# First layer's beginning: a constant tile on TensorE, the first context in four loads, two query groups behind the first scores

## The chip, the core and the metric

The kernel runs on one core of one Trainium2 chip. A core has several engines that run side by side, each with its own queue of instructions: TensorE (PE in the profile; its weight loads are listed apart as PEld), VectorE (DVE), ScalarE (ACT), GpSimd (POOL), and SyncE (SP), which in this kernel issues the transfers (DMAs). They hand over to one another by semaphores. Matrix products go from SBUF, the on-chip memory, to PSUM, a set of banks from which ACT and DVE copy the results out. The metric is the device time of one execution in microseconds (us); the shorter the better.

## The reference

Four layers follow one another on `x` of 8 batches, 100 rows and 512 columns, with a context of 8 batches, 361 rows and 512 columns. Only the first layer's head matters here. The first layer is an attention with 32 query heads of 16 columns and 8 key heads, each of which serves four query heads:

```python
q = hidden_state @ Wq + bq
k = encoder_hidden_state @ Wk + bk
v = encoder_hidden_state @ Wv + bv
q = q.reshape(b, l, KVH, GROUPS, HD).transpose(0, 2, 3, 1, 4)
...
scores = jnp.einsum('bkgld,bksd->bkgls', q, k) * scale
scores = scores + encoder_attention_mask[:, :, None, :, :]
attn = jax.nn.softmax(scores, axis=-1)
out = jnp.einsum('bkgls,bksd->bkgld', attn, v)
...
out = out @ Wo + bo
x = out + hidden_state
```

A normalization of the rows ends the layer. Layer 2 is a recurrent one, layer 3 a second attention, layer 4 two more attentions and two dense products. All values are 32-bit floats.

## The kernel before

**The loop.** The first layer walks over the eight batches `b`. In each it walks over seven row tiles `t` (`row_tiles`, six of 115 rows and one of 110). The 800 rows of a batch are, for one half of the key heads after the other, 4 query groups of 100 rows: row `r` belongs to group `r % 400 // 100`. So row tile 0 (rows 0 to 114) holds rows of groups 0 and 1, row tile 1 (115 to 229) of groups 1 and 2, and row tile 2 (230 to 344) of groups 2 and 3.

**The pieces, by function.**

- `context(b)` (L235) issues the load of a batch's context, turned so that its columns lie on the partitions: tile `cx`, four chunks of 128 columns in one DMA (L238, 722 KB). For `b == 0` it issues the query weights `wq` as well (the helper `load`, L91, 1024 KB) and the first 200 columns of the turned input, `xT` (L247, 400 KB).
- `keys(b)` (L251) multiplies the four chunks of `cx` with the key weights `wk`, one chunk after the other, into the PSUM tile `pk`; ACT writes the result with its bias to `kT` (L255).
- `queries(b, g)` (L289) makes one query group for two batches from `wq` and `xT` in the PSUM tile `pq`. ACT writes the half for the even key heads (L300), DVE that for the odd ones (L301), both into the tile `qz`. The even half is rows 0 to 399, the odd half rows 400 to 799.
- `masks(b)` (L303) issues the mask's rows for all seven row tiles. A row tile runs over the end of a head's 100 rows, so each takes two DMAs (L312). There are six buffers for the seven tiles.
- `key_values(b)` (L257) makes the values: three row blocks of `cx` times the weights `wv`, into the PSUM tile `pw`, with the bias `bv` added by DVE (L281). For `b == 0` it also issues a string of loads: `wv` (256 KB), `bv`, the second context, the rest of `xT` (L265, 1200 KB), the rows `x` (L269), `wo` and three row vectors.
- `scores(b, t, qz)` (L318) makes four score tiles `sc` of one row tile, one for each pair of key heads (L325). They have four PSUM banks.
- `softmaxed` (L333) adds the mask and finds the row minimum of the negated scores on DVE (L337), and takes exponentials on ACT (L341).
- `turned` (L344) transposes the exponentials of the row tile before on TensorE (`pt`, L349); the copies to `at` are ACT's for three of the four pairs (L229) and DVE's for the fourth (L231). The transposes have two PSUM banks.
- `values` (L377) multiplies the exponentials with the values and finishes the rows.

**What sets the order.** Within `tc.manual_schedule` (L451) the engines PE, DVE and ACT keep the order in which the program calls them. SP and POOL are not listed: a planner places their instructions when the program is built. All DMAs of the head go through SP's one queue. They use eight semaphores in turn, and an issue waits until the DMA that had its semaphore before has landed, that is the eighth before it.

**The head's order on TensorE.** `keys(0)`; `queries(0, 0)` to `queries(0, 3)`; then, in the loop for `b == 0`: the scores of row tile 0, the values' product (`key_values(0)`), the scores of row tile 1, the transposes of row tile 0, the scores of row tile 2, and so on. At `t == 2` and `t == 6` come query groups of the next two batches. The PSUM tiles `pk`, `pq`, `pw` and some later ones share a tag, "av", with two banks.

A matrix product of 32-bit floats appears in the trace as two instructions: the four products of `pk` are listed as x8, the sixteen of the four query groups as x32.

Of the kernel before, what the change touches and what calls it, by code (L numbers as in the profile page):

```python
# [10 lines left out]
F32 = mybir.dt.float32  # L11
# [5 lines left out]
P = 128  # L17
B, L, C, S = 8, 100, 512, 361
T = B * L
NC = C // P  # L20
# [36 lines left out]
def kernel(ctx: ExitStack, tc: tile.TileContext, d: dict, out: bass.AP):  # L57
    nc = tc.nc
# [20 lines left out]
    def row_bcast(dst, name, parts, lo=0, n=None):  # L79
        at, size = RV_AT[name]  # L80
        n = size if n is None else n
        nc.sync.dma_start(out=dst, in_=d["rvec"][0:1, at + lo : at + lo + n].to_broadcast([parts, n]))
# [5 lines left out]
    def load(pool, name, k, n, tag, lo=None):  # L88
        t = pool.tile([P, k, n], F32, tag=tag, name=tag)
        src = d[name] if lo is None else d[name][:, lo : lo + n]  # L90
        nc.sync.dma_start(out=t, in_=src.rearrange("(c p) n -> p c n", p=P))  # L91
        return t
# [108 lines left out]
    with ExitStack() as es:  # L201
        p1 = es.enter_context(tc.tile_pool(name="l0_1", bufs=1))
        p2 = es.enter_context(tc.tile_pool(name="l0_2", bufs=2))
        p4 = es.enter_context(tc.tile_pool(name="l0_4", bufs=4))
        ps = es.enter_context(tc.tile_pool(name="l0_ps", bufs=2, space=PSUM))
# [3 lines left out]

        keys3 = (0, KB, S - KB)  # L210

        wk = load(p1, "L0_xattn_Wk", NC, P, "wk")
        qmask = p1.tile([P, 2], F32, tag="qmask", name="qmask")
        nc.sync.dma_start(out=qmask, in_=d["qmask"])
# [8 lines left out]
        wv = bv = wq = wo = xT = bo = gamma = beta = None  # L223
# [11 lines left out]
        def context(b):  # L235

            cx = p2.tile([P, NC, S], F32, tag="cx", name="cx")
            nc.sync.dma_start(  # L238
                out=cx, in_=d["ctxT"][:, b * S : (b + 1) * S].rearrange("(c p) s -> p c s", p=P)
            )  # L240
            contexts[b] = cx
            nonlocal wq, xT
            if b == 0:
                wq = load(wpool, "L0_xattn_Wq", NC, C, "w")
                xT = p1.tile([P, NC, T], F32, tag="xT", name="xT")
                rows = d["xT"].rearrange("(c p) t -> p c t", p=P)
                nc.sync.dma_start(out=xT[:, :, : 2 * L], in_=rows[:, :, : 2 * L])  # L247
            if b == 2:
                factors.extend(load(wpool, f"L2_xattn_w_{j}", NC, C, "w") for j in "qk")

        def keys(b):  # L251
            cx = contexts[b]
            pk = ps.tile([P, 512], F32, tag="av", name="pk")
            mm_sum(pk[:, :S], [(wk[:, c, :], cx[:, c, :]) for c in range(NC)])
            nc.scalar.activation(kT[:, b, :], pk[:, :S], AF.Identity, bias=col("L0_xattn_bk", 0), scale=1.0)  # L255

        def key_values(b):  # L257
            cx = contexts.pop(b)
            nonlocal wv, bv, wo, bo, gamma, beta
            if b == 0:  # L260
                wv = load(p1, "L0_xattn_Wv", NC, P, "wv")
                bv = p1.tile([P, P], F32, tag="bv", name="bv")
                row_bcast(bv, "L0_xattn_bv", P)
                context(1)
                nc.sync.dma_start(  # L265
                    out=xT[:, :, 2 * L :], in_=d["xT"].rearrange("(c p) t -> p c t", p=P)[:, :, 2 * L :]
                )
                for i in range(B):
                    nc.sync.dma_start(out=x[i], in_=d["x"][i])  # L269
                wo = load(wpool, "L0_xattn_Wo", NC, C, "w")  # L270
                bo = p1.tile([L, C], F32, tag="bo", name="bo")
                row_bcast(bo, "L0_xattn_bo", L)
                gamma = p1.tile([L, C], F32, tag="gamma", name="gamma")
                row_bcast(gamma, "L0_xattn_gamma", L)
                beta = p1.tile([L, C], F32, tag="beta", name="beta")
                row_bcast(beta, "L0_xattn_beta", L)
            pw = ps.tile([P, 512], F32, tag="av", name="pw")
            for k, lo in enumerate(keys3):
                mm_sum(pw[:KB, k * P : (k + 1) * P], [(cx[:, c, lo : lo + KB], wv[:, c, :]) for c in range(NC)])
            for k in range(3):  # L280
                nc.vector.tensor_tensor(  # L281
                    v[:, b, k, : 8 * HV].rearrange("p (h e) -> p h e", e=HV)[:, :, :16],
                    pw[:KB, k * P : (k + 1) * P].rearrange("p (h e) -> p h e", e=16),
                    bv[:KB].rearrange("p (h e) -> p h e", e=16),
                    ALU.add,
                )
            nc.gpsimd.memset(v[: 3 * KB - S, b, 2, :], 0.0)
# [15 lines left out]
        def masks(b):  # L303

            tiles = []
            for r0, n in row_tiles:
                mk = p2.tile([QR, S], F32, tag="mask", name="mask", bufs=6)
                tiles.append(mk)
                done, lo = 0, r0 % L
                while done < n:  # L310
                    m = min(n - done, L - lo)
                    nc.sync.dma_start(  # L312
                        out=mk[done : done + m], in_=d["mask_Bx1xSxS2_ff0"][b, 0, lo : lo + m]
                    )
                    done, lo = done + m, 0
            return tiles

        def scores(b, t, qz):  # L318
# [106 lines left out]
        def advance():  # L425
            for g in list(steps):
                try:
                    next(g)
                except StopIteration:
                    steps.remove(g)  # L430
# [19 lines left out]
        ordered = {mybir.EngineType.PE, mybir.EngineType.DVE, mybir.EngineType.Activation}  # L450
        with tc.manual_schedule(engines=ordered):  # L451
            context(0)
            keys(0)
            for g in range(4):
                queries(0, g)
            before = None

            for b in range(B):
                mk = masks(b)
                ats = [p2.tile([KB, 3, PROWS], F32, tag="at", name="at", bufs=4) for _ in range(NPAIR)]  # L460
                y = p2.tile([L, C], F32, tag="y", name="y", bufs=1)
                for t in range(len(row_tiles)):
                    banks = scores(b, t, qzs[b - b % 2])
                    prs = []
                    if t == 1 and b > 0:
                        prs = [softmaxed(t, banks[p], mk) for p in range(NPAIR)]
                        last = values(b - 1, 1, *late)
                        next(last)
                        start(last)
                    copies = []  # L470
                    if before is not None:
                        copies = [turned(before[0], p, before[1][p], before[2][p]) for p in range(2)]
                        for copied in copies:
                            copied()
                    prs = prs or [softmaxed(t, banks[p], mk) for p in range(NPAIR)]
                    if b > 0:
                        next(adding, None)
                    advance()
                    if t == 0:
                        key_values(b)  # L480
                        if 0 < b < B - 1:
                            context(b + 1)
                    if t == 4 and b + 1 < B:
                        keys(b + 1)
                    if t in (2, 6) and b - b % 2 + 2 < B:
                        queries(b - b % 2 + 2, b % 2 * 2 + t // 6)
                    if before is not None:
                        for p in range(2, NPAIR):
                            turned(before[0], p, before[1][p], before[2][p])()
                    before = (t, prs, ats)  # L490
                    if b == B - 2 and t == 6:
                        first_rows()
                    if t == 4:
                        start(values(b, 0, ats, y))
                late = (ats, y)
            for p in range(NPAIR):
                if p == 0:
                    fold_chunk(0, *factors, wqk_d, ps.tile([P, 512], F32, tag="av", name="pf"), p2)
                turned(before[0], p, before[1][p], before[2][p])()
            start(values(B - 1, 1, *late))  # L500
            while steps:
                advance()
            assert len(added) == 2
# [6 lines left out]
    with ExitStack() as es:  # L510
        p1 = es.enter_context(tc.tile_pool(name="l1_1", bufs=1))
        pb = es.enter_context(tc.tile_pool(name="l1_2", bufs=2))
        ps = es.enter_context(tc.tile_pool(name="l1_ps", bufs=2, space=PSUM))
# [470 lines left out]
        with tc.manual_schedule(engines=L1_ORDERED):  # L984
# [11 lines left out]
            for n in range(NU * STEPS + 1):  # L996
                u, c, i = n // STEPS, n % STEPS // 4, n % 4
# [33 lines left out]
                if n == 3 * STEPS - 3:  # L1031
# [4 lines left out]
                    for src in (wqk_d, wvo_d):  # L1036
                        t = wpool.tile([P, NC, C], F32, tag="w", name="w")
# [19 lines left out]
    ps = ctx.enter_context(tc.tile_pool(name="l3_ps", bufs=2, space=PSUM))  # L1057
# [589 lines left out]
```

## Time and profile before

| what | value |
|---|---|
| runs of the kernel | 2767.51, 2770.15 and 2777.99 us, median 2770.15 |
| the profiled execution | 2770.51 us |
| its span, first to last instruction | 2768.7 us, 40339 instructions |
| TensorE's busy share of the span | 96% |
| first matmul | starts at 8.53 us |
| first query product | starts at 13.32 us |
| first scores | start at 18.87 us |

Times within the profile count from the first instruction. The span is a little shorter than the execution's own time. A row of the timeline gives the start of a group of equal instructions, how long it lasted, the engine, the line, the operation, the tiles written and read, and the number of instructions; in brackets stands how long the engine was idle before it, and what ended that. A wait for several semaphores is put down to the one that came last, and since DMAs share semaphores, the DMA that is named there can be another one of the same semaphore.

SP's issues of the head, from the timeline (start us, us):

```profile
0.74 0.41 SPq L66 DMA_DIRECT2D pv<-in_pvec  x1
1.20 0.42 SPq L82 DMA_DIRECT2D alpha<-in_rvec  x1
1.66 0.43 SPq L91 DMA_DIRECT2D wk<-in_L_xattn_Wk  x1
2.13 0.51 SPq L214 DMA_DIRECT2D qmask<-in_qmask  x1
2.68 0.43 SPq L238 DMA_DIRECT2D cx<-in_ctxT  x1
3.16 0.51 SPq L91 DMA_DIRECT2D w<-in_L_xattn_Wq  x1
3.71 0.51 SPq L247 DMA_DIRECT2D xT<-in_xT  x1
4.26 11.07 SPq L312 DMA_DIRECT2D mask<-in_mask_Bx1xSxS_ff  x12
15.37 0.40 SPq L91 DMA_DIRECT2D wv<-in_L_xattn_Wv  x1
15.81 0.51 SPq L82 DMA_DIRECT2D bv<-in_rvec  x1
16.37 0.43 SPq L238 DMA_DIRECT2D cx<-in_ctxT  x1
16.84 0.51 SPq L265 DMA_DIRECT2D xT<-in_xT  x1
21.86 0.68 SPq L312 DMA_DIRECT2D mask<-in_mask_Bx1xSxS_ff  x2
```

The first seven DMAs have the queue to themselves. Twelve mask DMAs follow, spread over 11 us, then those of `key_values(0)`; the seventh row tile's masks stand last, as their buffer comes free with the first row tile.

### The profile page before, as it was taken

How to read it: one execution, taken by the hardware profiler on the slowest of the kernel's cores; microseconds unless marked ns; L12 is line 12 of the kernel's file. 1: busy time of each engine (PE TensorE's matmuls, PEld its weight loads, DVE VectorE, ACT ScalarE, POOL GpSimd, SP SyncE). 2: the span in 40 equal slices, each digit the busy share in tenths (PEclk: the TensorE clock that was granted, in tenths of full speed). 3: DMA queues.
4: the chain of work that ended last, by engine and by line, in shares of the span. 5: the costliest groups of instructions: out<-in, count | busy, mean ns of one | idle time of the engine just before them, and what ended most of it. 6: DMA issues, size and time to landing. Idle time of an engine off the chain costs nothing.

```text
span 2768.7 us, 40339 instructions
## 1 busy us (share of the span) xinstructions
PE 2668.2 (96%) x14572; PEld 2147.3 (78%) x14572; DVE 1459.1 (53%) x3779; ACT 964.1 (35%) x2224; POOL 843.8 (30%) x1090
## 2 busy tenths in 40 slices
PE   8999889898989999999999999999999999999999
PEld 5666566675667899877799987789987789997688
DVE  4788367877425544436544436544444754443733
ACT  5777344553312333321333330233340133332211
POOL 2000144532103223255322236222326332324312
PEclk9999989999999999999999999999999999999999
DMA  7432433254205100045200025300005410004300
GB/s 226 122 101 69 146 101 116 89 149 132 64 5 155 42 23 22 7 112 149 69 22 23 1 63 156 110 19 22 12 11 144 133 48 22 22 4 132 126 13 13
DMA packets 142745, 207.52 MB, mean 75 GB/s; under 512 B 44910, under 2 KB 78158, under 8 KB 142290
## 3 DMA queue, kind: packets, MB, share of 16 engines
q1 hardware_dynamic: 142546, 204.94, 25.7%
q8 instruction: 116, 1.90, 0.3%
q14 instruction: 83, 0.68, 0.1%
HBM read 199.29 MB, written 5.61 MB: 74 GB/s over the span
## 4 chain that ended last, share of the span: by engine, by line
PE 73%; DVE 3%; ACT 1%; issue 1%; POOL 0%; DVEq 0%; POOLq 0%; ACTq 0%
PE pz L96 20%; PE sl L96 9%; PE su L96 6%; PE pk L1152 6%; PE pa L96 6%; PE pq L96 5%; PE po L1336 5%; PE pp L96 4%; PE pu L96 3%; PE pt L1267 2%; PE pl L96 2%; PE sc L96 2%; PE po L96 0%; PE pe L96 0%; DVE st L744 0%
## 5 line engine op out<-in xcount | busy, mean ns | idle before, releaser
L96 PE MATMUL pz<-at,cr 121*128 121x248 f32 (+3 forms) x2688 | 579.7, 358 | 0.0
L96 PEld LDWEIGHTS pz<-at,cr 121*128 121x128 f32 (+1 forms) x2688 | 471.0, 189 | 42.3 <-ACT at L1270 3.4
L1216 POOL TENSOR_TENSOR ss<-qz 128x248 f32<-128x248 f32 x96 | 68.1, 709 | 631.4 <-PE su L96 487.1
L1152 PE MATMUL pk<-q,wb 128*128 128x400 f32 x512 | 189.9, 501 | 1.1 <-PE pq L96 1.1
L750 POOL TENSOR_TENSOR st<-st,r 128x800 f32<-128x800 f32 x64 | 112.0, 1750 | 236.0 <-DVE st L744 199.0
L96 PE MATMUL pa<-qz,wa 128*128 128x400 f32 x512 | 178.8, 500 | 0.0
L1301 ACT ACTIVATE pr<-su,nm 124x362 f32<-124x362 f32 x96 | 54.1, 564 | 328.4 <-DVE nm L1298 328.4
L96 PE MATMUL sl<-ts,ss 128*124 128x181 f32 x768 | 155.6, 324 | 0.3
L1079 DVE COPY qz<-pz 128x496 f32<-128x496 f32 (+1 forms) x112 | 70.9, 633 | 139.7 <-PE pz L96 139.0
L96 PEld LDWEIGHTS pa<-qz,wa 128*128 128x128 f32 x512 | 95.5, 190 | 63.0
L1077 ACT COPY qz<-pk 128x400 f32<-128x400 f32 x128 | 63.0, 492 | 231.1 <-PE pk L1152 231.1
L96 PEld LDWEIGHTS sl<-ts,ss 128*124 128x124 f32 x768 | 116.8, 186 | 19.4 <-issue 11.4
L1152 PEld LDWEIGHTS pk<-q,wb 128*128 128x128 f32 x512 | 93.5, 190 | 48.5 <-ACT qz L1077 3.7
L1270 ACT COPY at<-pt 121x372 f32<-121x372 f32 (+1 forms) x208 | 89.0, 473 | 113.3 <-PE pt L1267 113.1
L349 PEld LDWEIGHTS pt<-ident,pr 115*121 115x121 f32 (+1 forms) x672 | 83.2, 185 | 56.5 <-ACT at L229 29.2
L744 DVE TENSOR_TENSOR_SCAN st<-wd,a 128x808 f32<-128x808 f32 x64 | 117.1, 1830 | 15.2 <-PE py L755 13.4
L1077 ACT COPY qz<-pz 128x496 f32<-128x496 f32 (+1 forms) x112 | 60.5, 540 | 183.2 <-PE pz L96 182.7
L1306 ACT ACTIVATE pr<-pr,ss 124x362 f32<-124x362 f32 (+1 forms) x208 | 118.3, 594 | 8.7 <-DVE ss L1304 7.8
L341 ACT ACTIVATE pr<-pr,nm 115x361 f32<-115x361 f32 (+1 forms) x224 | 115.2, 592 | 10.4 <-DVE nm L337 10.4
L1121 DVE TENSOR_TENSOR tu<-sl,tu 124x181 f32<-124x181 f32 x96 | 33.4, 348 | 157.4 <-PE sl L96 157.3
L1372 DVE TENSOR_TENSOR aT<-pa,u 128x400 f32<-128x400 f32 x64 | 36.8, 575 | 142.5 <-PE pa L96 123.7
L337 DVE CUSTOM_DVE_ANT_0 pr<-sc,mask 115x361 f32<-115x361 f32 (+1 forms) x224 | 106.1, 531 | 11.0 <-PE sc L325 10.8
(360 smaller groups left out, 5640.6 us busy)
## 6 DMA issues: line engine op xcount, KB each, us to landing
va<-vd SPq DMA_DIRECT2D x64, 404.0 KB
wa<-in_L_xattn_wq SPq DMA_DIRECT2D x64, 256.0 KB
wb<-in_L_xattn_wk SPq DMA_DIRECT2D x64, 256.0 KB
wa<-in_L_xattn_wv SPq DMA_DIRECT2D x64, 256.0 KB
wb<-in_L_xattn_wo SPq DMA_DIRECT2D x64, 256.0 KB
u<-pd SPq DMA_DIRECT2D x64, 200.0 KB
cr<-in_ctxR SPq DMA_DIRECT2D x16, 726.0 KB
cx<-in_ctxT SPq DMA_DIRECT2D x16, 722.0 KB
```

The lines of the kernel that those rows point to most:

```text
L96: nc.tensor.matmul(dst, lhsT=lt, rhs=r, start=(i == 0), stop=(i == len(pairs) - 1))
L337: nc.vector.tensor_tensor_reduce(out=pr[:n], in0=sc[:n, :S], in1=mk[t][:n], scale=-1.0, scalar=FLT_MAX, op0=ALU.add, op1=ALU.min, accum_ou ...
L341: nc.scalar.activation(pr[:n], pr[:n], AF.Exp, bias=nm[:n], scale=-1.0)
L349: nc.tensor.transpose(pt[:KB, k * n : (k + 1) * n], pr[:n, lo : lo + KB], ident[:n, :n])
L744: nc.vector.tensor_tensor_scan(st.rearrange("p q b l -> p (q b l)"), wd.rearrange("p q t -> p (q t)"), a, 0.0, ALU.mult, ALU.add,)
L750: nc.gpsimd.tensor_tensor(st, st, rc.unsqueeze(1).to_broadcast([P, 4, UB, L]), ALU.mult)
L1077: nc.scalar.copy(o, i)
L1079: nc.vector.tensor_copy(o, i)
L1152: nc.tensor.matmul(pk[:, :HT], lhsT=wk[:, c * P : (c + 1) * P], rhs=q, start=True, stop=True)
L1270: nc.scalar.copy(at[:, :, o : o + r], pt[:KB, : 3 * r].rearrange("p (k r) -> p k r", r=r))
L1306: nc.scalar.activation(pr[:r, : S + 1], pr[:r, : S + 1], AF.Copy, scale=ss[:r])
L1336: nc.tensor.matmul(po[:, c], lhsT=left[k][:, c * P : (c + 1) * P], rhs=right[k], start=True, stop=True)
```

## The change

Four edits, all in the first layer.

1. A tile `ones` of 128 by 128 is filled by DVE, and TensorE multiplies it with itself 16 times (`WARM`) into a PSUM tile of the tag "av", between `context(0)` and `keys(0)`. Nothing reads the result.
2. `context(0)` loads the first context in four DMAs, one for each chunk of 128 columns, where there was one. Later contexts keep one DMA.
3. `wv` and `bv` are issued in `masks(0)`, behind the DMAs of the first row tile and ahead of those of the second, where they stood in `key_values(0)` behind all masks.
4. Only query groups 0 and 1 are made ahead of the loop. Group 2 is made in row tile 0 and group 3 in row tile 1, each behind the row tile's own softmax in the program's order: on TensorE group 2 stands between the scores of row tile 0 and the values' product, and group 3 between the first and the second half of the transposes of row tile 0; on ACT and DVE their evictions stand behind the softmax of row tile 0 and of row tile 1.

```diff
+        WARM = 16
+        ones = p1.tile([P, P], F32, tag="ones", name="ones")
+        nc.vector.memset(ones, 1.0)
         wk = load(p1, "L0_xattn_Wk", NC, P, "wk")
...
-            nc.sync.dma_start(
-                out=cx, in_=d["ctxT"][:, b * S : (b + 1) * S].rearrange("(c p) s -> p c s", p=P)
-            )
+            src = d["ctxT"][:, b * S : (b + 1) * S].rearrange("(c p) s -> p c s", p=P)
+            for c in range(0, NC, 1 if b == 0 else NC):
+                cs = slice(c, c + 1 if b == 0 else NC)
+                nc.sync.dma_start(out=cx[:, cs], in_=src[:, cs])
...
             if b == 0:
-                wv = load(p1, "L0_xattn_Wv", NC, P, "wv")
-                bv = p1.tile([P, P], F32, tag="bv", name="bv")
-                row_bcast(bv, "L0_xattn_bv", P)
                 context(1)
...
                     done, lo = done + m, 0
+                if wv is None:
+                    wv = load(p1, "L0_xattn_Wv", NC, P, "wv")
+                    bv = p1.tile([P, P], F32, tag="bv", name="bv")
+                    row_bcast(bv, "L0_xattn_bv", P)
...
             context(0)
+            pk = ps.tile([P, 512], F32, tag="av", name="warm")
+            for _ in range(WARM):
+                nc.tensor.matmul(pk[:, :P], lhsT=ones, rhs=ones, start=True, stop=True)
             keys(0)
-            for g in range(4):
+            for g in range(2):
                 queries(0, g)
...
                     if b > 0:
                         next(adding, None)
+                    elif t < 2:
+                        queries(0, t + 2)
                     advance()
```

More of the change, by code (lines that the diff above doesn't have):

```diff
@@ L258, in key_values @@
             cx = contexts.pop(b)
-            nonlocal wv, bv, wo, bo, gamma, beta
+            nonlocal wo, bo, gamma, beta
             if b == 0:
-                wv = load(p1, "L0_xattn_Wv", NC, P, "wv")
-                bv = p1.tile([P, P], F32, tag="bv", name="bv")
-                row_bcast(bv, "L0_xattn_bv", P)
                 context(1)
@@ L305, in masks @@
             tiles = []
+            nonlocal wv, bv
             for r0, n in row_tiles:
```

## The prediction

> **What bounds the kernel, and the head of it.** I read the page first (busy shares), then a table of stages, then the head's timeline, engine by engine. Page, then stages (us; busy time of PE, PEld, DVE, ACT, POOL with instruction counts; granted clock; DMA share; GB/s):
>
> ```profile
> PE 2668.2 (96%) x14572; PEld 2147.3 (78%) x14572; DVE 1459.1 (53%) x3779; ACT 964.1 (35%) x2224; POOL 843.8 (30%) x1090
> ...
> 0.00:24.00 24.00, 15.47 (x86) 11.83 (x86) 5.50 (x22) 6.07 (x11) 4.00 (x8) 1.00 0.77 236
> 24.00:40.00 16.00, 14.20 (x96) 9.80 (x96) 9.59 (x36) 13.29 (x30) 0.00 (x0) 1.00 0.77 237
> 40.00:310.00 270.00, 253.77 (x1895) 164.86 (x1893) 202.41 (x866) 187.10 (x408) 11.44 (x15) 1.00 0.36 103
> ```
>
> TensorE bounds the whole. The change touches only the first 31 us or so. In the first 24, PE idles 8.53; from 24 to 40 ACT is the busiest after PE (13.29 of 16) and PE idles 1.8. So more than about 10 us cannot be won, and whatever is won early must pass 24 to 31 us, where PE waits for ACT. PE's timeline there (start, us, what; in brackets idle before it):
>
> ```profile
> 8.53 4.95 PE L96 MATMUL pk<-cx,wk 128*128 128x361 f32 x8 [8.53 <-DMA cx<-in_ctxT]
> 13.32 5.63 PE L96 MATMUL pq<-xT,w 128*128 128x200 f32 x32
> 18.87 0.88 PE L325 MATMUL sc<-kT,qz 32*115 32x361 f32 x8
> 19.68 2.88 PE L96 MATMUL pw<-wv,cx 128*121 128x128 f32 x24
> 22.49 0.88 PE L325 MATMUL sc<-kT,qz 32*115 32x361 f32 x8
> ...
> 25.26 0.95 PE L325 MATMUL sc<-kT,qz 32*115 32x361 f32 x8
> 27.04 0.89 PE L349 MATMUL pt<-ident,pr 115*121 115x115 f32 x6 [0.83 <-ACT at L229]
> ```
>
> The same `pk` group takes 2.61 us at 35.59, so at 8.53 it ran at half speed (0.60 us a matmul for 0.33). The clock's own record begins at 13.15 with full speed; the 1.00 in rows before that is no measurement.
>
> **The gate that the page hides.** Do the queries follow `pk` because `pk` is late, or because their inputs are? PE's weight loads, then what SP's queue waited for between 4 and 14 us:
>
> ```profile
> 13.17 1.01 PEld L96 LDWEIGHTS pq<-xT,w 128*128 128x128 f32 x6 [0.56 <-DMA mask<-in_mask_Bx1xSxS_ff]
> ...
> SPq L312 <- DMA w<-in_L_xattn_Wq: 2.5, 1, 2.5
> SPq L312 <- DMA xT<-in_xT: 1.5, 1, 1.5
> ```
>
> The first query weight waited 0.56 us for a DMA. It is named a mask, but queries read no mask. DMAs share eight semaphores in turn, each issue waiting for the one eight before it; SP's mask issue that waited for `xT` went out at 13.09. In the semaphore records `cx` lands from 6.76 (fastest of 16 engines) to 8.39, `Wq` at 11.23, **`xT` at 13.07**. Both bounds meet at 13.1: `pk`'s end and `xT`'s landing.
>
> **Constant tile.** 16 matmuls are 32 instructions (16 query matmuls are x32). DVE is free at 0.9; I estimate PE's start at 1.2 (a 128x128 memset took POOL 0.21). Cold, 128 columns cost 0.60*128/361 = 0.21 us each; warm 2.88/24 = 0.12. Bounds: 3.8 to 6.8 us, end 5.0 to 8.0. Before, full speed came 13.15 - 8.53 = 4.6 us after the first matmul: so 22 cold (4.6), 10 warm (1.2), end 7.0: the block does not reach the landing of the queries' inputs at 13.1. Its memset stands ahead of DVE's wait for `qmask` (5.05) and costs nothing. `pk` then costs 2.6, saving 4.95 - 2.6 = 2.3 us.
>
> **Four loads.** 180 KB each, SP 0.43 to 0.51 us an issue: `Wq` goes out near 4.7 for 3.16, `xT` near 5.2 for 3.71. Here a rule speaks against the change. By row: `Wq` (1024 KB) landed 11.23 - 8.39 = 2.84 us after `cx`, 369 GB/s, so neighbours in the queue overlap and pay no fixed cost each; chunks land about 6.2 to 8.4, and `Wq` and `xT` keep 11.2 and 13.1, as their bytes queue behind the same bytes and their issues still lead. By the Trainium skill, "DMA: Bandwidth & Descriptors", section Anatomy of one DMA (stated for GpSimd's DMAs), each DMA has about 2 us fixed: three more would put the last chunk at an estimated 14.4 and the first query some 2 us late, 2772.6. I take the row. `pk` ends at 8.4 + 2*0.33 = 9.1 (bounds: 8.7, or 11 with a late constant block).
>
> **What is late next: `xT`.** PE idles 9.1 to 13.1, and queries start at 13.1 for 13.3: 0.2 gained of the 4. Cost of the idle: by row, one gap of 3.21 us in this trace put the clock at half for the next 3.4:
>
> ```profile
> 306.90:310.10 3.20, 0.05 (x1) 0.00 (x0) 2.25 (x13) 1.21 (x4) 0.00 (x0) 1.00 0.13 34
> 310.10:313.50 3.40, 3.34 (x4) 1.50 (x5) 0.72 (x3) 3.38 (x7) 1.68 (x2) 0.50 1.00 285
> ```
>
> That gap began at 306.95; clock changes lie on a raster of 3.41 us (the record's shortest stretch), with the change at 310.11, so nearly a whole step must be idle. A step fits whole into 4.0 us in (4.0 - 3.4)/3.4 = 18% of phases. By the Trainium skill, "TensorE: Matmul & The Clock Gate", section Why this matters for your kernels, any gap over about 3 us falls to half: then the queries lose 3.4/2 = 1.7 us, 2772.3. I take the row: no drop, 2770.6.
>
> **Two groups behind the scores.** Rows 0 to 114 need groups 0 and 1; a group is 5.63/4 = 1.4 us. Queries 13.1 to 15.9. New wait: `sc` needs group 1's eviction, which before hid behind groups 2 and 3: 0.15 start plus 0.52 on ACT, 0.1 signal: 0.75 (bounds 0.7, or 1.2 if DVE's 0.48 counts too). Behind it on PE stand group 2 and `pw`. Scores 16.7 to 17.5 (2.2 earlier), group 2 to 18.9, `pw` to 21.65, second scores 21.65 for 22.49: **0.84 won here, with group 3 still owed**. Then the evictions, ACT as it was:
>
> ```profile
> 23.91 0.80 ACT L229 COPY at<-pt 121x345 f32<-121x345 f32 x2 [1.35 <-PE pt L349]
> 24.59 2.06 ACT L341 ACTIVATE pr<-pr,nm 115x361 f32<-115x361 f32 x4
> 26.55 0.43 ACT L229 COPY at<-pt 121x345 f32<-121x345 f32 x1
> 27.65 0.80 ACT L229 COPY at<-pt 121x345 f32<-121x345 f32 x2 [0.66 <-PE pt L349]
> ```
>
> Moved 0.84 ahead, the copies run 23.05 to 23.85 and the exponentials end at 25.8. Group 3's eviction (0.52) stands behind them by program order, to 26.3, and the third scores (rows 230 to 344) wait for it: **26.35 for 25.26**. They end at 27.15; the transposes that stood at 27.04 start then. ACT's later copy moves to 26.3, so it isn't in the way. DVE's third softmax starts near 27.35 for 26.25, ends near 29.2; ACT's next exponentials began at 28.33, and the first row minima suffice for that. Sum at the transposes: +0.1. With DVE's wait instead, +0.6; with the scores free of group 3, -0.3.
>
> **Loads moved.** `wv` and `bv` go ahead of mask tiles 1 to 5, on SP: two issues and 320 KB, 0.9 us later for ten mask DMAs. Tile 1's masks landed at 15.1 and are first read near 22.4: hidden. `wv` landed at 18.27; now behind `xT` and 166 KB of mask, 422 KB at 369 GB/s after 13.07, about 14.3; wanted at 18.9. Without the move 0.6 us would still be left. The second `cx` and the rest of `xT` stand as far back in bytes; the latter landed at 26.82 and is wanted near 28: 1.2 us of cover, then each us late costs one. Mask tile 6 waits for the first softmax, `x` loads behind it: both 2 us earlier, unneeded until 40.56. POOL's queue only loses a wait.
>
> **Sum.** The profiled execution took 2770.51 around its span of 2768.7; +0.1 is 2770.6. The runs' median is 2770.15, 0.36 below it, well inside their scatter (2767.51 to 2777.99).
>
> **Rivals, with chances.**
> - *Forecast, 0.45*: `xT` and ACT take the gain back; 2770.6, own range 2770 to 2771.5.
> - *The gain survives, 0.20*: `xT` lands much earlier once it stands behind smaller loads, queries at 9.2 for 13.3, a gain of 4.1, less the third scores' loss of 0.3 to 1.1: 2767. For it: PE has 4 us of room. Against: DMA is at 363 GB/s from 5 to 10 us, no hole to fill.
> - *Clock falls, slower, 0.25*: the gap before the queries; 2772.3, up to 2774 with two steps at half. Decides from 3.2 us of idle over a whole step. For it: the gap of 4.0. Against: the constant block may end at 8 and `pk` at 10 to 11, leaving 2 to 3.
> - *Something far behind moves, 0.10*: DVE, ACT and POOL have no order written from 310 us on, and the clock there averages 0.90 over 530 us; 3% of that stage is 16 us, either sign: 2755 or 2787. No row speaks for it.
>
> The range reaches over the first three and the scatter of runs: 2765 to 2777. I call 0.5% (13.9 us) what this kernel's measurement can tell from nothing. The first three cases all lie within it: same 0.88; the last and odd scatter leave slower 0.07, faster 0.05.
>
> **What would show it.** Right: `pk` warm and ended before 10, a PE gap ended by a DMA at 12.8 to 13.4, first scores near 16.7, second near 21.7, third after 26, with ACT's `qz` just before. Wrong: queries before 12 (the gate was `pk`), a query group of 2.5 us or more (clock fell), third scores before 25 (ACT had room), or a stage after 310 us that differs by over 10.

## The result, and the profile after

| | before | after |
|---|---|---|
| median of five runs each, us | 2770.15 (2767.51 to 2777.99) | 2782.15 (2776.45 to 2784.23) |
| ratio, with its 95% interval | | 1.0036 [1.0022, 1.0051] |
| two later series of the same kernels, ratio | | 1.0014 [1.0005, 1.0023] and 1.0018 [1.0008, 1.0029] |
| profiled execution: own time, span | 2770.51, 2768.7 | 2784.23, 2782.4 |
| mean granted clock of that execution | 0.981 | 0.978 |

The change made the kernel slower, by 0.1 to 0.4%: all three intervals leave 1 out. The median of the first five runs, and four of the five, lie above the forecast range of 2765 to 2777. The 42 later runs of the same kernel have a median of 2774.3 and a mean of 2775.5, inside the range; the medians of their two series are 2.9 and 4.1 us above the kernel before beside them. Both parts have to be explained: what the change costs as a rule, and why the first series showed three times as much.

TensorE's timeline after (start us, us, what; in brackets the idle time before it), and, last, the second batch's `pk` before:

```profile
1.11 6.57 PE L462 MATMUL warm<-ones 128*128 128x128 f32 x32 [1.11 <-DVE ones L215]
7.52 2.60 PE L96 MATMUL pk<-cx,wk 128*128 128x361 f32 x8
14.14 4.40 PE L96 MATMUL pq<-xT,w 128*128 128x200 f32 x16 [4.03 <-DMA xT<-in_xT]
19.15 0.88 PE L332 MATMUL sc<-kT,qz 32*115 32x361 f32 x8 [0.61 <-ACT qz L302]
19.96 1.62 PE L96 MATMUL pq<-xT,w 128*128 128x200 f32 x8
...
28.75 0.88 PE L332 MATMUL sc<-kT,qz 32*115 32x361 f32 x8 [0.93 <-ACT qz L302]
...
38.12 2.61 PE L96 MATMUL pk<-cx,wk 128*128 128x361 f32 x8
```

```profile
35.59 2.61 PE L96 MATMUL pk<-cx,wk 128*128 128x361 f32 x8
```

The first two stages that the prediction shows for the kernel before, in the execution after (stretch, length, busy time of PE, PEld, DVE, ACT, POOL with instruction counts, granted clock, DMA share, GB/s):

```profile
0.00:24.00 24.00, 18.25 (x96) 16.20 (x96) 3.97 (x16) 5.34 (x9) 3.78 (x7) 0.93 0.70 198
24.00:40.00 16.00, 14.32 (x99) 10.32 (x99) 10.51 (x40) 12.18 (x28) 0.28 (x2) 1.00 0.83 278
```

TensorE is busier in the first 24 us, 18.25 for 15.47, and yet later at their end: 6.57 us of that is the constant tile, and the clock averages 0.93 (its record begins at 6.87 us; what stands before counts as full). The constant tile did what it was built for: `pk` takes 2.60 us for 4.95 and ends at 10.1. Then TensorE waits 4.03 us for `xT`, and the first query starts at 14.14 where it had started at 13.32. Eight query instructions took 1.4 us before; here sixteen take 4.40. The third scores stand at 28.75 for 25.26, the next `pk` at 38.12 for 35.59: **2.5 us are lost by 40 us**. SP's issues, then the clock around the gap (columns as above):

```profile
2.68 1.85 SPq L245 DMA_DIRECT2D cx<-in_ctxT  x4
4.58 0.43 SPq L91 DMA_DIRECT2D w<-in_L_xattn_Wq  x1
5.05 0.51 SPq L252 DMA_DIRECT2D xT<-in_xT  x1
...
10.30:13.70 3.40, 0.00 (x0) 0.00 (x0) 0.00 (x0) 0.42 (x1) 0.00 (x0) 1.00 1.00 293
13.70:17.10 3.40, 2.96 (x9) 2.99 (x10) 0.00 (x0) 0.00 (x0) 0.00 (x0) 0.50 0.63 172
17.10:20.00 2.90, 2.29 (x18) 1.47 (x16) 0.97 (x2) 1.04 (x2) 0.00 (x0) 1.00 0.72 176
```

On ACT, group 3's eviction stands where it was expected, between the exponentials and the next copy, and the third scores start when it is done:

```profile
26.23 2.06 ACT L348 ACTIVATE pr<-pr,nm 115x361 f32<-115x361 f32 x4
28.19 0.51 ACT L302 ACTIVATE qz<-pq,qb,qmask 128x200 f32<-128x200 f32 x1
28.59 0.45 ACT L233 COPY at<-pt 121x345 f32<-121x345 f32 x1
```

`xT` landed at 14.01 for 13.07 (the semaphore records), and the clock ran at half for one step of 3.41 us just as the queries came. The rest of the loss lies between 290 and 860 us. From 40 to 290 us each matmul stays 2.5 us behind its twin of before; by 860 it is 13.5 behind; from there to the end 13.5 to 14.3. TensorE has the same products in the same order there, and DVE, ACT and POOL take the same time for their work (from 300 to 860 us, DVE 372.8 and 373.0, ACT 223.5 and 223.5, POOL 186.0 and 185.8 us in sum of durations). What differs is the clock: 116.1 us at half between 290 and 860 us, for 102.4. From the second `pk` to layer 4's first product, before and then after (columns as above):

```profile
35.59:836.28 800.69, 723.29 (x4473) 508.77 (x4471) 526.66 (x1325) 392.06 (x799) 182.10 (x127) 0.94 0.35 105
```

```profile
38.12:849.19 811.07, 728.87 (x4473) 513.29 (x4471) 527.92 (x1330) 392.59 (x799) 181.89 (x127) 0.93 0.36 104
```

Of the 10.4 us between them, 5.6 are longer busy time of TensorE, which is what the clock takes directly: 13.7 us more at half speed can cost 6.8 at most. The other 4.8 are longer waits of TensorE, spread over the stage; whether these follow from the clock too was not shown. The first place where the two part shows the same products before and then after. Above each stands the raster step that decided (the clock changes only at steps of 3.41 us):

```profile
296.40:299.87 3.47, 2.35 (x9) 1.14 (x10) 0.39 (x1) 1.77 (x2) 0.00 (x0) 1.00 0.00 0
...
298.05 3.68 PE L96 MATMUL po<-w,yT 128*100 128x512 f32 x8 [0.58 <-ACT yT L408]
```

```profile
297.00:300.40 3.40, 1.48 (x9) 0.76 (x8) 0.68 (x2) 0.89 (x2) 0.00 (x0) 1.00 0.00 0
...
300.54 5.29 PE L96 MATMUL po<-w,yT 128*100 128x512 f32 x8 [0.58 <-ACT yT L415]
```

The same eight matmul instructions, with the same wait before them, take 1.6 us more. Before, they fell into a step that was 2.35 us busy, and the clock stayed full; after, the step ended just ahead of them with 1.48 us busy, and half clock followed.

### The profile page after: what moved, and what is told of

It is laid out like the page before. It is cut to its first block, busy times and chain, and to the rows that moved or that the text cites. A ratio compares the mean times of both kernels' runs of the same rounds, so it can differ in the third digit from the quotient of the medians.

```text
span 2782.4 us, 40408 instructions
## 1 busy us (share of the span) xinstructions
PE 2679.9 (96%) x14604; PEld 2159.0 (78%) x14604; DVE 1459.7 (52%) x3780; ACT 964.1 (35%) x2224; POOL 842.0 (30%) x1090
## 4 chain that ended last, share of the span: by engine, by line
PE 84%; DVE 7%; ACT 4%; DMA 1%; issue 1%; SPq 1%; POOL 1%; DVEq 0%; ACTq 0%; POOLq 0%
PE pz L96 20%; PE sl L96 9%; PE su L96 6%; PE pk L1164 6%; PE pa L96 6%; PE pq L96 6%; PE pp L96 5%; PE po L1348 5%; PE pu L96 3%; PE pt L1279 2%; PE pl L96 2%; PE pt L356 2%; PE sc L96 2%; PE po L96 2%; DVE st L756 2%
## 5 line engine op out<-in xcount | busy, mean ns | idle before, releaser
L96 PEld LDWEIGHTS sl<-ts,ss 128*124 128x124 f32 x768 | 116.8, 186 | 19.8 <-issue 11.6
L756 DVE TENSOR_TENSOR_SCAN st<-wd,a 128x808 f32<-128x808 f32 x64 | 117.0, 1828 | 18.3 <-PE py L767 15.1
L348 ACT ACTIVATE pr<-pr,nm 115x361 f32<-115x361 f32 (+1 forms) x224 | 115.3, 592 | 10.9 <-DVE nm L344 10.9
```

The costliest lines, as they stand in the source:

```text
L96: nc.tensor.matmul(dst, lhsT=lt, rhs=r, start=(i == 0), stop=(i == len(pairs) - 1))
L348: nc.scalar.activation(pr[:n], pr[:n], AF.Exp, bias=nm[:n], scale=-1.0)
L756: nc.vector.tensor_tensor_scan(st.rearrange("p q b l -> p (q b l)"), wd.rearrange("p q t -> p (q t)"), a, 0.0, ALU.mult, ALU.add,)
```

## The experiments

All ratios are to the kernel before, run beside the experiment. The place "at 40 us" is the start of the second batch's `pk`: 35.59 us in the first profile of the kernel before, 36.11 in its second.

### The two kernels again

Both without an edit, to see what repeats.

> The kernel before, unchanged, as a second sample of its clock record. Theory A (the head lost 2.5 us to the clock; the other 10 us, between 290 and 860 us, are where the clock's raster of 3.41 us happened to fall, not the change): ratio 1.000, but the total time at half clock in its profile differs from the 102 us of the first one by 5 to 15 us, and the time between 290 and 860 us with it. Theory B (the change itself makes the stage from 290 us on slower): half-clock total 102 within 4 us again, as nothing was changed.

> The changed kernel, unchanged, as a second sample. Theory A: ratio 1.001 to 1.003, the half-clock total lies anywhere from 95 to 120 us, and the head differs from the first profile if the raster falls elsewhere (first scores near 17.5 us when the clock stays full through the gap, near 19.1 when it falls). Theory B: ratio 1.0036 or more, half-clock total again near 119 us.

> The changed kernel a third time. Its first five runs had a median of 2782.15, the next 22 one of 2774.73. Theory A (the head's 2.5 to 3.5 us, and scatter of the clock's raster behind it): median 2773 to 2777 beside a kernel before near 2771.5, third scores at 27.2 to 29.7, xT near 14.0, and a half-clock total behind 290 us anywhere from 95 to 120 us. Theory B (something in the stage behind makes it 10 us longer as a rule): median above 2779.

Measured: the kernel before again, ratio 0.9999 [0.9990, 1.0009], 109.2 us at half clock, and the time from its second `pk` to layer 4's first product 804.6 us for 800.7. The changed kernel, medians 2774.73 (22 runs) and 2773.56 (20 runs), ratios in the table above; half clock behind 290 us 112.6 and 95.6 us; `xT` at 14.11 and 14.27; third scores at 29.72 and 30.17, a little later than I expected, since the clock stayed at half for two steps (query groups 5.26 and 5.56 us); at 40 us 39.08 and 39.53.

What follows: the head's loss repeats, 2.5, 3.5 and 3.9 us over the first profile of before, half a microsecond less over its second. The time from the second `pk` to layer 4 does not belong to the version: 811, 806 and 799 us in the three profiles of the changed kernel. Over 19 profiles of 14 versions, with the same order of products on TensorE in all, it runs from 797 to 811 us, and correlates with the time at half clock there (0.89). The 13.7 us by which the first two profiles differ are 2.5 of the head and some 11 of that stage. Each run's mean clock agrees: all 36 runs at or over 2780 us, of any version, have a mean granted clock of 0.979 or less, and over the 251 later runs of the kernel before time and clock correlate with -0.80.

### A bridge over the gap

Sixteen more products of the constant tile (`BRIDGE = 16`) between the keys and the first query.

```diff
             keys(0)
+            pk2 = ps.tile([P, 512], F32, tag="av", name="warm2")
+            for _ in range(BRIDGE):
+                nc.tensor.matmul(pk2[:, :P], lhsT=ones, rhs=ones, start=True, stop=True)
             for g in range(2):
```

> The changed kernel with 16 more products of the constant tile between the keys and the first query, some 3.8 us at full clock, so that TensorE is busy while it waits for xT. Theory A: the clock stays full, the two query groups take 2.8 us for 4.4, first scores at 17.5 and third scores near 26.5 to 27.2 for 28.75; 1.7 us faster than the changed kernel at 40 us, ratio to the kernel before about 1.0003 plus the scatter of the later stage. Theory B: the same gain in the head, but the stage from 290 us on stays 10 us longer, ratio 1.003. Rival for the head: if the clock was not the cause, the query groups stay at 4.4 us.

TensorE's timeline of this version:

```profile
14.02 2.94 PE L96 MATMUL pq<-xT,w 128*128 128x200 f32 x16 [0.74 <-DMA xT<-in_xT]
17.57 0.88 PE L332 MATMUL sc<-kT,qz 32*115 32x361 f32 x8 [0.61 <-ACT qz L302]
```

Nothing was changed for `xT` (13.88), and the two groups take 2.94 us: the clock was the cause of the 1.5 to 2.6 us that they lose in the changed kernel. At 40 us it is 36.53, 0.9 late for the first profile of before and 0.4 for the second. What is left is the late `xT` in the main: the first query starts 0.7 later than in the first profile of before. Ratio 1.0011 [1.0000, 1.0022].

### One part alone, or one part undone

**Only the query groups behind the scores** (edit 4), and **only four loads** (edit 2).

```diff
-            for g in range(4):
+            for g in range(2):
                 queries(0, g)
...
+                    elif t < 2:
+                        queries(0, t + 2)
```

```diff
-            nc.sync.dma_start(
-                out=cx, in_=d["ctxT"][:, b * S : (b + 1) * S].rearrange("(c p) s -> p c s", p=P)
-            )
+            src = d["ctxT"][:, b * S : (b + 1) * S].rearrange("(c p) s -> p c s", p=P)
+            for c in range(0, NC, 1 if b == 0 else NC):
+                cs = slice(c, c + 1 if b == 0 else NC)
+                nc.sync.dma_start(out=cx[:, cs], in_=src[:, cs])
```

> The kernel before with one part of the change alone: query groups 2 and 3 behind the first and second scores. No constant tile, one load of the context, wv where it was. Theory A: first scores near 16.7 for 18.87, second scores 21.7 if wv (18.3) is there in time, third scores 26.3 for 25.26 because they wait for group 3's eviction; at 40 us within 0.5 us of the kernel before. Rival: the third scores hold back what follows and it is 1 us late at 40 us. Half-clock total from 95 to 120 us by theory A, near 102 by theory B unless this part is what B rests on.

> The kernel before with the context in four loads alone. In five profiles so far xT landed at 13.07, 13.18 and 13.27 us with one load and at 14.01, 14.11 and 13.88 with four. Theory A: the three more issues put Wq's issue 1.4 us later and with it the landing of xT, so xT lands near 14.0 and Wq near 12.5 again; keys start near 6.5 at half clock, end near 11.4, and the first query starts near 14.1, some 0.7 later than before. Rival (the constant tile or the loads of wv and bv behind xT delay it): xT lands near 13.2.

The timeline with the moved groups alone, then with four loads alone:

```profile
17.77 0.88 PE L325 MATMUL sc<-kT,qz 32*115 32x361 f32 x8 [0.61 <-ACT qz L300]
...
27.36 0.88 PE L325 MATMUL sc<-kT,qz 32*115 32x361 f32 x8 [0.93 <-ACT qz L300]
28.17 0.89 PE L349 MATMUL pt<-ident,pr 115*121 115x115 f32 x6
```

```profile
6.14 5.15 PE L96 MATMUL pk<-cx,wk 128*128 128x361 f32 x8 [6.14 <-DMA cx<-in_ctxT]
14.59 7.38 PE L96 MATMUL pq<-xT,w 128*128 128x200 f32 x32 [3.30 <-DMA xT<-in_xT]
```

The moved groups: first scores 1.1 us earlier, third 2.1 later, each held by ACT's `qz`; the transposes behind them at 28.17 for 27.04, at 40 us 36.73. That is 1.1 late for the first profile of before and 0.6 for the second, which started its queries at 13.81 like this one; half a microsecond of it is the clock, which here turned full only at 14.8. Ratio 0.9999 [0.9987, 1.0010]. The rival was right in that the third scores wait, but little is passed on. `wv`, not moved here, landed near 18.3 and `pw` followed the queries at 20.03 without idle time: here **moving `wv` would have bought nothing**.

Four loads alone: `xT` at 14.45, the keys start 2.4 us earlier than before, a gap of 3.30, and the queries at half clock. At 40 us 38.61, 3.0 us late. One profile only, one time of 2771.97.

**One load again**, the other edits kept, and **the constant tile alone**:

```diff
-            for c in range(0, NC, 1 if b == 0 else NC):
-                cs = slice(c, c + 1 if b == 0 else NC)
-                nc.sync.dma_start(out=cx[:, cs], in_=src[:, cs])
+            nc.sync.dma_start(out=cx, in_=src)
```

> The changed kernel with the context in one load again; constant tile, early wv and bv, and the moved query groups stay. Theory A: xT lands near 13.2, the keys run at full clock from 8.5 to 11.1, the gap before the first query is 2.2 us for 4.0 to 4.9, so the clock stays full, first query near 13.3, first scores near 16.8 and third near 26.4; at 40 us within 0.5 us of the kernel before, ratio 1.000. Rival (a gap of 2 us is enough to lose the clock, or early wv and bv delay xT): query groups of 2 us and more each, or xT at 14.

> The kernel before with the constant tile alone. Theory A: keys at full clock from 8.6 to 11.3, the first query waits for xT until 12.7 to 13.3 with 1.5 to 2 us of idle, clock full, first scores near 18.4 to 18.9, at 40 us within 0.5 us of the kernel before; ratio 1.000. Beside it a question that the runs raised: of 93 runs of kernels with the constant tile 15 were at or over 2780 us, of 126 without it 2. Theory C (the early products make the clock's raster behind 290 us fall worse): 10 to 20% of the runs at or over 2780. Theory A has no reason for that: 2%.

```profile
8.62 2.67 PE L96 MATMUL pk<-cx,wk 128*128 128x361 f32 x8 [2.28 <-DMA cx<-in_ctxT]
12.82 2.95 PE L96 MATMUL pq<-xT,w 128*128 128x200 f32 x16 [1.52 <-DMA xT<-in_xT]
16.37 0.88 PE L330 MATMUL sc<-kT,qz 32*115 32x361 f32 x8 [0.61 <-ACT qz L300]
...
25.96 0.88 PE L330 MATMUL sc<-kT,qz 32*115 32x361 f32 x8 [0.92 <-ACT qz L300]
```

That is the timeline with one load. `xT` is back at 12.68, the gap is 1.52 us, the clock stays full, and at 40 us it is 35.33: the loss is gone. From the second `pk` to layer 4 this version takes 798.7 us. Ratio 1.0001 [0.9985, 1.0018]. The constant tile alone: `pk` ends at 11.5, then 1.77 us of waiting for `xT` (13.09), first scores at 18.86 for 18.87, at 40 us 35.58 for 35.59; ratio 0.9998 [0.9990, 1.0007]. So **the tile alone is worth nothing, because `xT` is the gate; the four loads do the harm, by `xT` and by the gap they open.**

**The constant tile undone**, twice, and **the tile filled but its products left out**; the other edits stay.

> The changed kernel without the constant tile and its products; four loads, early wv and bv, and the moved query groups stay. Theory A: keys at half clock from 6.1 to 11.3 as in the run with four loads alone, then a gap of about 3 us to xT near 14.2, queries at half clock (two groups 4 us or more), at 40 us 2 to 3.5 us later than the kernel before, ratio 1.001. Theory C: no more than 3% of the runs at or over 2780. Theory D (memory placement or the moved groups cause the long runs): 10 to 20%.

> The changed kernel with the tile filled, in its place in memory, but without the 16 products. Theory A: as without the tile, 2 to 3.5 us late at 40 us, ratio 1.001. Theory C: no more than 3% of the runs at or over 2780. Theory D (memory placement): 10 to 20%.

> The changed kernel without the tile, a second time. Theory F: again no long run or one at most, median near 2773, 2 to 3 us above the kernel before for the head. Theory A: about as many as for the changed kernel, 3 to 5 of 22.

Without products the keys run at half clock from about 6, end between 11.0 and 11.8, and gaps of 2.5 to 2.8 us follow. The clock fell in all three, and the two groups took 4.62, 4.63 and 4.30 us. At 40 us 38.27, 37.97 and 38.20. Ratios 0.9999 [0.9989, 1.0009], 1.0016 [1.0004, 1.0028] and 1.0007 [0.9999, 1.0015]. The clock of the second run without the tile, and then of the version with the tile alone, around their gaps (columns as above):

```profile
12.30:15.70 3.40, 1.37 (x8) 1.40 (x9) 0.00 (x0) 0.07 (x1) 0.00 (x0) 1.00 0.68 167
15.70:19.10 3.40, 2.94 (x10) 2.40 (x8) 0.48 (x1) 0.94 (x2) 0.00 (x0) 0.51 0.62 180
```

```profile
11.00:14.40 3.40, 1.63 (x9) 1.20 (x8) 0.00 (x0) 0.56 (x1) 0.00 (x0) 1.00 0.60 152
14.40:17.80 3.40, 3.40 (x22) 3.27 (x21) 0.97 (x2) 1.22 (x3) 0.00 (x0) 1.00 0.71 196
```

A step that was busy for 1.37 of 3.40 us (40%) is followed by half clock, one with 1.63 (48%) is not. The second was lucky: by the count in the last section most steps that are so little busy are followed by half clock, and with one load (55%) the full clock was not certain either.

### A version meant to beat both

The constant tile, one load of the context, all groups ahead; `Wq` in two loads with `xT` between them, and `alpha` behind the first layer's loads:

```diff
-                wq = load(wpool, "L0_xattn_Wq", NC, C, "w")
+                wq = wpool.tile([P, NC, C], F32, tag="w", name="w")
+                wsrc = d["L0_xattn_Wq"].rearrange("(c p) n -> p c n", p=P)
+                nc.sync.dma_start(out=wq[:, :, : 2 * P], in_=wsrc[:, :, : 2 * P])
...
                 nc.sync.dma_start(out=xT[:, :, : 2 * L], in_=rows[:, :, : 2 * L])
+                nc.sync.dma_start(out=wq[:, :, 2 * P :], in_=wsrc[:, :, 2 * P :])
```

> A version meant to beat both: the kernel before with the constant tile, one load of the context, all four query groups ahead of the scores, Wq in two loads (columns of groups 0 and 1 ahead of xT, those of groups 2 and 3 behind it), and alpha, which layer 3 needs first, issued behind the first layer's loads. Theory A says that xT's landing is the gate: 512 KB less ahead of it at 369 GB/s is 1.4 us, alpha's 128 small packets up to 1 us more, so xT lands at 10.8 to 11.8, keys end near 10.5 to 11.1 and first scores start near 16.8 to 17.4 for 18.87, second scores near 20.5 to 21; 1.5 to 2.1 us gained at 40 us, ratio 0.9993. Rival: the gain is lost again between 24 and 31 us, where ACT is busiest, and less than 0.5 us is left at 40 us.

> The version with Wq in two loads again, for a narrower interval. Its profile gained 2.4 us at 40 us. Theory A: xT near 10.0, first scores near 15.8, 2 to 2.5 us gained at 40 us again, and a ratio of 0.999 to 1.000, at the edge of what the scatter lets one see. Theory C: 10 to 20% of its runs at or over 2780, as it has the early products (0 of 12 so far).

```profile
7.61 2.67 PE L95 MATMUL pk<-cx,wk 128*128 128x361 f32 x8 [0.65 <-DMA cx<-in_ctxT]
10.13 5.70 PE L95 MATMUL pq<-xT,w 128*128 128x200 f32 x32
15.76 0.88 PE L331 MATMUL sc<-kT,qz 32*115 32x361 f32 x8
```

`xT` lands at 9.99 and 10.42, 2.9 us earlier than with one `Wq` load on average; 1.4 of that was counted for the bytes, and `wk` in front comes 0.8 and 0.4 earlier (4.00 and 4.36 for 4.77) without `alpha`; the rest was not taken apart. The queries follow the keys without idle time, and at 40 us it is 33.23 and 33.43: **2.2 to 2.9 us won over the two profiles of before, and kept through the stretch where ACT is busiest**. Only here did `wv` hold TensorE up: it landed at 17.22 and 17.41, and `pw` waited 0.7 and 0.5 us for it. An early `wv` was not tried with this version. The time doesn't show it: ratios 1.0003 [0.9994, 1.0012] and 0.9998 [0.9986, 1.0009]. 2.4 us are 0.09%, and the kernel before alone scatters from 2762.97 to 2782.01 over 251 runs.

### The runs at or over 2780 us

The changed kernel had 7 of them among its 42 later runs, the kernel before 3 of 251. Is it an edit?

> The kernel before with wv and bv issued behind the first row tile's masks, and nothing else. Theory E (the early loads make long runs): 10 to 25% of the runs at or over 2780 us, though the head is within 0.5 us of the kernel before at 40 us. Theory A (long runs are chance): at most 3%. Both: xT near 13.1, first scores near 18.9, ratio within 0.999 to 1.002.

> The changed kernel with wv and bv back in their old place. Theory E: no more than 3% of the runs at or over 2780, median near 2773 to 2774, as the head's 2.4 to 3.9 us stay (xT near 14.1, clock at half in the queries). Theory A: 15% at or over 2780 as for the changed kernel, or as few as for any other, by chance.

> The kernel before with early wv and bv and the moved query groups; no tile, one load. Head as with the moved groups alone: xT near 13.1, at 40 us 0.1 to 1.2 us later than the kernel before. Theory E: 10 to 25% of the runs at or over 2780. If only this version and not the early loads alone has long runs, both edits together are needed; if neither has, the tile's memory has a part in it.

> The kernel before with the tile filled (no products) and the moved query groups; one load, wv and bv where they were. Theory F (the tile's place in memory together with the moved groups makes long runs): about 20% of the runs at or over 2780 us, 3 to 5 of 22, though the head is as with the moved groups alone, 0.1 to 1.2 us late at 40 us. Theory A (chance): at most 1 of 22.

Measured, at or over 2780: early `wv` alone 2 of 22, `wv` back in its place 6 of 22, early `wv` with the moved groups 0 of 14, tile filled with the moved groups 2 of 22. From the runs above: bridge 3 of 22, one load 2 of 12, tile filled only 7 of 22; moved groups alone 0 of 14, tile alone 0 of 22, without the tile 0 of 14 and 1 of 22, the version with `Wq` in two loads 0 of 26. The early loads (theory E) and the products (theory C) are refuted: without the one there are 6 of 22, without the other 7 of 22. That the filled tile and the moved groups together do it (theory F) fits the list but not well the test made for it, 2 of 22 where 3 to 5 were expected, and early `wv` alone, which has neither, had 2 as well. **This stays open.** Ratios: 1.0006 [0.9997, 1.0014], 1.0016 [1.0006, 1.0026], 0.9997 [0.9988, 1.0007], 1.0010 [1.0000, 1.0019].

## Why the prediction was wrong

- **The gate was right.** `xT` ends the wait, `pk` at full clock gains nothing, and the gap is the 4.0 us worked out, though both of its ends came a microsecond late. The constant block took 6.57 us for the 5.8 worked out: the clock's record begins 5.76 us after the first product, where the prediction had taken 4.6 from one trace (2.96 to 6.03 over 19 profiles). Nothing hangs on that here.
- **"Four loads ... keep 11.2 and 13.1": wrong.** The step took landings as set by bytes alone. `xT` landed at 12.68 to 13.39, mean 13.1, in eight profiles with one load, and at 13.63 to 14.45, mean 14.1, in nine with four: 1.0 us. `Wq` in front of it was late already, 12.1 to 12.8 for 10.9 to 11.6. From 6 to 10 us the DMAs moved 356 to 381 GB/s with one load (373 before) and 257 to 349 with four (286 after). The Trainium skill's fixed cost of 2 us for each DMA ("DMA: Bandwidth & Descriptors", Anatomy of one DMA, stated for GpSimd's DMAs) was far too much for these, three more cost 1 us together; but it pointed the right way. Whether the later issue of `Wq` (4.58 for 3.16) or the small loads leave the holes was not separated.
- **"I take the row: no drop": wrong, and this is the step that failed.** From one gap of 3.21 us I inferred that a raster step must be idle as a whole, and gave it 18%. One idle step that is followed by half clock shows that this is enough, not that it is needed. The same trace held the answer: of its 15 falls from full clock 13 came behind steps that were 26 to 75% busy, as this one, 2.04 of 3.42 us:

```profile
361.30:364.72 3.42, 2.04 (x20) 1.30 (x20) 2.93 (x3) 3.41 (x9) 1.74 (x1) 1.00 0.43 146
364.72:368.10 3.38, 2.11 (x12) 1.10 (x12) 3.38 (x4) 3.23 (x7) 2.47 (x2) 0.50 0.48 141
```

In the first profile of the changed kernel a whole step was idle (10.3 to 13.7), the prediction's own 18%. But the clock fell in all four profiles of the changed kernel with its `wv` early or late, and in four more with gaps of 2.5 to 3.3 us; in six of the eight the step before was 10 to 41% busy. It cost 1.4 to 2.7 us in the two query groups, where the rival said 1.7. A gap of 4.0 us leaves one of the steps that it touches idle for at least 2.0 of 3.4 us wherever the raster falls, so by the count in the last section the fall was nearly certain. The rule that I set aside, the Trainium skill's gap of about 3 us ("TensorE: Matmul & The Clock Gate", Why this matters for your kernels), gave the right answer, though gaps of 2.47 to 2.76 us were enough here.
- **The moved groups were right in shape, and near in size.** With one load and the tile, from the first query to the next `pk` it is 22.51 us with the moved groups and early loads and 22.35 without: +0.16. The prediction's times give +0.3 for the same stretch (13.1 to 27.15 for 13.32 to 27.04); its sum of +0.1 has the earlier first query in it. Start of the scores to the third scores: 9.6 us, as worked out (16.7 to 26.35). That the early gain is taken back at ACT was right.
- **Early `wv`: nothing, as predicted.** SP's planner also put the rest of `xT` behind the seventh row tile's masks (issue 22.68 for 16.84), which I had not foreseen. That comes with the moved groups (21.31 with them alone), not with early `wv` (16.90 alone); the query that needs it came late enough.
- **The range.** The sum with the two wrong steps put right is 2770.5 + 1.0 + 2.0 + 0.1, about 2773.6, near the 2774.3 of the later runs and still inside the range; the rival "clock falls" at 2772.3 had the mechanism of the head. What carried the first series 8 us higher, and out of the range, is the stage from 290 to 860 us: 11 us in its profiled run, and the mean clock of all five runs, 0.978 or 0.979, speaks for the same in the others. The prediction's last sign of being wrong, "a stage after 310 us that differs by over 10", all but came: 9.4 of the 11 us lie behind 310. The rival that named it had a chance of 0.10, and the range was drawn from the scatter of three runs (10.5 us), one of which, at 2777.99, lay outside it; over 251 runs the scatter is 19 us. That long runs are runs with more half clock is shown; why that series had so many of them is not.

## What to carry to other kernels

Before TensorE is sped up or kept warm at a kernel's start, find the landing that its second piece of work waits for: here the shorter keys only bought a longer wait, and the wait cost the clock. Order the loads by when each is first needed and cut the one in front of the gate, not the one that is already early; splitting the wrong load moved the gate back by 1 us. Where a gap can't be closed, fill it with products of a constant tile right up to the landing, not only ahead of the first data. And before a rule is drawn from one row of a trace, look at every other place of the trace where the same thing happened.

## What the runs showed of the hardware that was not expected

- **The clock needs far less than an idle step to fall.** Counted over the first 900 us of the 19 profiles, in raster steps of 3.41 us: of 116 steps at full clock in which TensorE was under 40% busy, all 116 were followed by half clock; between 40% and 50% 83 of 104; between 50% and 80% 96 of 467; above that 5 of some 3,700. Back to full it went only after steps at least 84% busy (all 300 returns), and not always at once: 143 steps at half clock that were as busy were followed by another at half. A stage with many waits, as the one from 310 to 840 us, where TensorE is 88% busy on average but under 80% in 34 of 156 steps (first profile of the kernel before), pays for this over and over.
- **The raster is not tied to the program, and it is not the whole story.** Its offset from the first instruction takes any value from 0.04 to 3.39 us over the profiles. The stage from the second `pk` to layer 4 takes 797 to 811 us with the same order of products. But the first profile of the changed kernel and the one with one load meet that stage at the same offset: both fall to half 262.3 us after the second `pk` and step alike for 95 us; then the one stays at half for four steps and the other for three, and they end at 811.1 and 798.7 us. What tips such a step was not found. On this kernel a gain of 2.4 us in the head did not show in the time of 12 and 14 runs; it can be read only from the head's own timeline.
